# Fixing the order of VectorE, ScalarE and GpSimd in two stages of a two-layer transformer kernel

## The chip, the cores and the metric

The kernel runs on one core of one Trainium2 chip. The core has a matrix engine (TensorE, PE in the profile, with its weight loads listed as PEld), a vector engine (VectorE, DVE), an activation engine (ScalarE, ACT), a general engine (GpSimd, POOL) and SyncE (SP), which issues most transfers. Every engine works through its own list of instructions in order; semaphores hold an instruction until what it needs is done. The metric is the device time of one execution in microseconds (us); the times before are 2042.14, 2020.98 and 2023.09, median 2023.09. They spread over 1%.

## The reference

The input `x` is 8 batch items of 512 tokens with 256 features. Two layers follow each other, each with a conditioning in front of its attention and of its feed-forward part:

```python
x = x + L0_attn(L0_cond(x, c), ...)        # modulated attention; biased causal attention, 16 heads
x = x + L0_ffn(L0_cond2(x, ids, ...), ...) # conditioning by tables and a small network; 8 experts, top 2
x = x + L1_attn(L1_cond(x, c), ...)        # adapter with weights from c; linear attention with exp features
x = x + L1_ffn(L1_cond2(x, c, ...), ...)   # weights from c; 8-bit product with a scale per token
```

The second conditioning of layer 0, cut to its core, and the routing of its experts:

```python
h = ln(x, pw_g[pid], pw_b[pid]); h = ln(h, cp_g[cid], cp_b[cid])
t = ln(x, tm_g[cid], tm_b[cid]); s = ln(x, ms_g[mid], ms_b[mid])
m, n, r = (x + mlp_ln(state) for each of three states)
cat = concat([w0*h, w1*t, w2*m, w3*n, w4*r, w5*s])
xc = ln(silu(cat @ W1 + b1) @ W2 + b2)
probs = softmax(xc @ Wr + br); p, e = top_k(probs, 2)
pos = (how many earlier tokens of the item chose the same expert); keep = pos < 80
buf[e, item, pos] += xc                    # 80 slots per expert and item
y = relu(buf @ W1[e] + b1[e]) @ W2[e] + b2[e]
out = sum over the two choices of p * keep * y[slot]
```

## The kernel before

Python code traces the whole program as a list of instructions; a planner then sorts each engine's instructions by what it expects of their readiness, subject to the data they need, and places the semaphores. Three things take freedom from it. Every matrix product goes through `pmm` or a transpose through `ptr`, and both tie each product to the one before it, so that PE runs in the order of the source everywhere. A few GpSimd and VectorE operations are told to keep their order among themselves (`tc.keep_in_program_order`). And the first stage calls `in_order`, which adds an ordering edge, without a semaphore, from each instruction of VectorE, ScalarE or GpSimd to the next one of the same engine in the traced list:

```python
def in_order(start):
    last = {}
    for i in nc.cur_bb.bb.instructions[start:]:
        if i.engine not in (DVE, Activation, Pool):   # names shortened
            continue
        if i.engine in last:
            tc.add_manual_dep(i, last[i.engine].name, ...)
        last[i.engine] = i
```

The program has four stages. `stage_a1` is the first conditioning and attention. `stage_a2` is the second conditioning and the routing. `stage_b` runs the eight experts. `stage_c` runs layer 1. Tokens lie 128 to a tile, so there are 32 tiles, four to a batch item.

`stage_a2` handles two tiles (a "unit") per pass of its loop, 16 units in all, and is pipelined by hand over passes `it` = 1 to 22. In pass `it`, unit u = it is normalized, v = it - 1 is transposed, w = it - 2 goes through the first product of the network, y = it - 3 through the second, z = it - 4 through the router's product. The source traces a pass in this order:

1. statistics of unit u (`bn`, lines 1194 and 1195), `turn(v, 0)`: eight transposes on PE of four tensors (the input, ss, hh, tt) and two ScalarE copies into `cat`;
2. `layer2(y)` on PE, then on VectorE the addition of the bias (xc, line 1388) and the statistics of xc;
3. `inverse`: ScalarE takes a square root (line 1200), VectorE the reciprocal (1201) and the negated mean nmr (1340);
4. `normalize(u)`: ScalarE makes xh (1328); GpSimd makes tt and ss (1331, 1332) and issues the next unit's gathers from the tables (1142) between them;
5. `layer1(w, 0)` on PE; the four scalings of xc on VectorE (1400, 1401);
6. `pathway(u)`: four VectorE operations make hh (1347, 1348), then their statistics and a second `inverse` with its own square root and reciprocal;
7. `logits_turn(z)`: PE transposes of xc and a ScalarE copy xcT (1244); `turn(v, 1)`;
8. in an even pass from 6 on, `choose`: thirteen small VectorE operations that pick the two experts of each token and make `r_M` (1275); in an odd pass from 7 on, `one_hot` for the first two tiles of a batch item (1309, 1310, two operations of 640 columns for a tile);
9. `layer1(w, 1)` on PE, `silu(w)` on ScalarE (1228);
10. `compartment(u)`: four VectorE operations finish hh (1358, 1359);
11. `logits(z)` on PE, and their addition lg on VectorE (1252);
12. in an even pass, `places`: a product with `r_M` on PE (pos_ps) and ten small VectorE operations (1291 to 1302), then `dispatch(·, 1)`; in an odd pass, `one_hot` for the other two tiles, then `dispatch(·, 0)`.

`dispatch` is eight products on PE, for each half of the slots one for each of the four tiles in turn, so that it needs all four one-hots of the item; ScalarE copies the result (1319). The transposes of `turn(v, i)` read the hh of tile i alone.

In front of the loop the first two units are done as a "lead"; it is traced after the first stage and runs beside its tail, and its gathers are tied behind operations of the first stage's last round.

`stage_c` loops over nine rounds. In one round, the front half of batch item b (adapter, projections, features kf and qf, key-value products) is interleaved with the back half of item b - 1 (attention's division, output product, the quantized product). What matters here: `kfeatures` applies exp on ScalarE and an addition on VectorE to four tiles (1710, 1711), `values` adds a bias to the products v_ps (cv, 1694), `z` quantizes one tile in six VectorE operations (1817 to 1825), `qfeatures` is like `kfeatures` (1725, 1726), `keyvalues_turned` copies one half on VectorE (1752) and one on ScalarE (1753), `turn_q` copies a transposed tile on ScalarE (qzT, 1832), and `acc` is the quantized product with its scaling (r, 1840). In these two stages `small` and `ps_o` tiles in PSUM come from pools of three and two, so that a product can wait for the release of an earlier one.

Of the kernel before, what the change touches and what calls it, by code (L numbers as in the profile page):

```python
# [45 lines left out]
def tile_kernel(ctx: ExitStack, tc: tile.TileContext, t, out):  # L46
# [1394 lines left out]
        nc.vector.tensor_tensor(gates[:, 1], gates[:, 1], keep[:, 1], ALU.mult)  # L1441

    with ExitStack() as sub:
        stage_a2(sub)

# [461 lines left out]
                g.acc(3)  # L1909

    with ExitStack() as sub:
        stage_c(sub)


def pack(i):
# [70 lines left out]
def build(nc, arrays, out_ap):  # L1986
    t = {k: nc.dram_tensor("in_" + k, a.shape, mybir.dt.from_np(a.dtype), kind="ExternalInput").ap()
         for k, a in arrays.items()}
    with tile.TileContext(nc) as tc:
        tile_kernel(tc, t, out_ap)  # L1990
# [12 lines left out]
```

## Time and profile before

| what | value |
|---|---|
| median of the runs (lowest to highest) | 2023.09 us (2020.98 to 2042.14) |
| profiled execution: its own time, and the span in it | 2027.99 us, 2025.8 us |
| busy over the span: PE, DVE, ACT, POOL | 1827.9 (90%), 1140.9 (56%), 744.3 (37%), 689.2 (34%) |
| mean granted PE clock | 0.938 |
| PE of the second conditioning | 1030 to 1318, 288 us: PE busy 272.5, DVE 245.8 |
| PE of the experts | 1318 to 1617, 299 us: PE busy 294.4, DVE 67.3 |
| PE of the last stage | 1617 to 2026, 409 us: PE busy 369.8, DVE 254.5 |

A busy share is a mean over stages with different limits, so the stages are read one by one. The profile's times come from one execution; its own time is 2.2 us more than the span from its first instruction to its last. A time in brackets behind an instruction is how long its engine stood idle in front of it and what ended that. The durations of consecutive VectorE rows overlap by some 0.08 us, so sums in the text go from start to start. The granted clock of PE is given as a share of full speed.

### The profile page before, as it was taken

Reading aid. Unit: us, or ns where it says so; the run is one execution under the profiler, and the core shown is the slowest. Engines: PE = TensorE matmul, PEld = TensorE weight load, DVE = VectorE, ACT = ScalarE, POOL = GpSimd, SP = SyncE. Lnnn points to the kernel's source line nnn. Section 1 sums busy time; section 2 is a strip of 40 time slices with the busy share of each in tenths; the row PEclk is TensorE's granted clock in tenths of the full one; section 3 lists DMA queues with packets and bytes.
Section 4 is the critical chain, followed back from the end, with each engine's and each line's share of the span. In section 5 each row is a group of like instructions: output and inputs, shape, how many; then the busy total and the mean of one; then the engine's idle time right before and its main releaser. Section 6 shows DMA issues by size and latency. Waiting matters only on the chain.

```text
span 2025.8 us, 46400 instructions
## 1 busy us (share of the span) xinstructions
PE 1827.9 (90%) x19638; PEld 1258.0 (62%) x19658; DVE 1140.9 (56%) x2646; ACT 744.3 (37%) x1444; POOL 689.2 (34%) x1071
## 2 busy tenths in 40 slices
PE   6789898988999898988689999999999889999997
PEld 3446566555656566555468788777777645555554
DVE  3455656555655556565569898622221246666666
ACT  3425344353545344344445445311110023333332
POOL 3324332333434332332277555000000244444422
PEclk7698899999999998998789999999999989999999
DMA  4110101111020101101254334222322211111100
GB/s 132 39 42 7 39 17 44 33 44 32 7 65 7 59 7 45 37 22 53 100 193 150 124 125 137 87 78 92 105 70 74 51 44 31 34 32 35 35 12 22
DMA packets 102107, 119.72 MB, mean 59 GB/s; under 512 B 45350, under 2 KB 82332, under 8 KB 101772
## 3 DMA queue, kind: packets, MB, share of 16 engines
q1 hardware_dynamic: 91660, 74.82, 12.0%
q0 software_dynamic: 10240, 41.95, 6.5%
q8 instruction: 154, 2.52, 0.5%
q14 instruction: 53, 0.43, 0.1%
HBM read 94.46 MB, written 22.27 MB: 58 GB/s over the span
## 4 chain that ended last, share of the span: by engine, by line
PE 36%; DVE 12%; ACT 2%; POOL 2%; issue 2%; DMA 1%; SPq 0%; POOLq 0%; ACTq 0%; DVEq 0%
PE h_ps L87 7%; PE y_ps L87 6%; PE qf_ps L87 2%; PE kv_ps L87 2%; PE k_ps L87 1%; PE wo_ps L87 1%; PE dsp L87 1%; PE q_ps L87 1%; PE z_ps L87 1%; DVE s L1194 1%; DVE o1h L1310 1%; PE kf_ps L87 1%; PE hid_ps L87 1%; PE down_ps L87 1%; PE v_ps L87 1%
## 5 line engine op out<-in xcount | busy, mean ns | idle before, releaser
L745 ACT ACTIVATE eo<-o 128x384 f32<-128x384 f32 x256 | 111.8, 489 | 282.1 <-PE o L87 226.7
L722 POOL TENSOR_SCALAR_AFFINE_SELECT ed<-ed 128x512 f32<-128x512 f32 x128 | 78.9, 639 | 339.4 <-ACT ed L721 339.2
L87 PE MATMUL h_ps<-bufT,w 128*128 128x320 f32 x512 | 141.9, 438 | 0.0
L87 PE MATMUL y_ps<-w,hT 128*128 128x256 f32 x640 | 139.4, 379 | 0.0
L87 PEld LDWEIGHTS y_ps<-w,hT 128*128 128x128 f32 x640 | 121.6, 190 | 17.4
L87 PEld LDWEIGHTS h_ps<-bufT,w 128*128 128x128 f32 x512 | 97.9, 192 | 43.7 <-DVE us L1557 3.4
L1529 ACT ACTIVATE hT<-h_ps,w_b 128x320 f32<-128x320 f32 x64 | 33.8, 527 | 245.8 <-PE h_ps L87 245.8
L1594 POOL MEMSET bn<- 128x512 f32 x1 | 0.5, 525 | 342.7 <-PE h_ps L87 342.7
L87 PE MATMUL hid_ps<-cat,wx 128*128 128x256 f32 x512 | 116.4, 381 | 0.0
L604 DVE SCALAR_TENSOR_TENSOR kts<-kt_ps,w_bkp,fk 128x512 f32<-128x512 f32 x32 | 24.0, 751 | 160.1 <-PE kt_ps L87 160.1
L87 PEld LDWEIGHTS hid_ps<-cat,wx 128*128 128x128 f32 x512 | 96.7, 192 | 12.8
L639 DVE TENSOR_REDUCE mx<-mx_d 128x4 f32<-128x512 f32 x128 | 82.4, 686 | 33.8 <-PE mx_d L87 29.8
L1531 DVE TENSOR_SCALAR hT<-h_ps,w_b 128x320 f32<-128x320 f32 x64 | 35.3, 551 | 114.9 <-PE h_ps L87 114.9
L87 PE MATMUL o<-qts,kts 32*128 32x128 f32 (+1 forms) x768 | 96.3, 346 | 0.0
L706 DVE TENSOR_TENSOR sd<-sd,wt 128x512 f32<-128x512 f32 x128 | 82.1, 687 | 16.7 <-PE sd L87 10.4
L87 PE MATMUL sd<-qt,ktc 32*128 32x128 f32 x1024 | 87.2, 305 | 3.3 <-ACT ed L721 3.3
L87 PE MATMUL o<-mt,onesb 32*128 32x384 bf16 (+2 forms) x384 | 59.0, 286 | 33.0 <-DVE mx L639 25.2
L87 PEld LDWEIGHTS sd<-qt,ktc 32*128 32x128 f32 x1024 | 71.7, 204 | 23.7 <-issue 16.8
L87 PE MATMUL sd<-qt,kts 16*128 16x128 f32 x1024 | 81.0, 294 | 0.0
L87 PEld LDWEIGHTS sd<-qt,kts 16*128 16x128 f32 x1024 | 70.9, 200 | 16.0 <-issue 15.5
L1538 DVE TENSOR_TENSOR ye<-y_ps,bc_b 128x256 f32<-128x256 f32 x40 | 17.0, 424 | 107.4 <-PE y_ps L87 107.4
L87 PEld LDWEIGHTS o<-qts,kts 32*128 32x128 f32 x768 | 75.9, 201 | 0.2
(423 smaller groups left out, 4596.6 us busy)
## 6 DMA issues: line engine op xcount, KB each, us to landing
w<-in_W SPq DMA_DIRECT2D x16, 1024.0 KB
xT<-in_xT SPq DMA_DIRECT2D x8, 512.0 KB
kxd<-kxF SPq DMA_DIRECT2D x8, 512.0 KB
raw<-kxd SPq DMA_DIRECT2D x64, 64.0 KB
xr<-in_x SPq DMA_DIRECT2D x8, 512.0 KB
ond<-on SPq DMA_DIRECT2D x64, 64.0 KB
oT<-ond SPq DMA_DIRECT2D x8, 512.0 KB
x1d<-xr SPq DMA_DIRECT2D x8, 512.0 KB
```

The source lines that it names most:

```text
L87: pin(nc.tensor.matmul(*a, **kw))
L604: nc.vector.scalar_tensor_tensor(kts.rearrange("p (j k) -> p j k", k=P), ps.rearrange("p (j k) -> p j k", k=P), bkp[:, g:g + 1], fk[:, g]. ...
L639: nc.vector.tensor_reduce(mx[:, g, 0:4], d[g].rearrange("p (j k) -> p j k", k=P), AX.X, ALU.max)
L706: nc.vector.tensor_tensor(d3, d3, wt[:, self.hg * 4 + g].unsqueeze(1).to_broadcast([P, NT, P]), ALU.mult)
L722: zeroed.append(nc.gpsimd.affine_select(e, e, pattern=[[0, NT], [1, P]], compare_op=ALU.is_ge, fill=0.0, base=0, channel_multiplier=-1))
L745: nc.scalar.activation(e, self.o[g][:, :3 * P], AF.Exp)
L1194: nc.vector.bn_stats(s6, x)
L1310: nc.vector.scalar_tensor_tensor(o1, slot, sd[:, 1, j:j + 1], o1, ALU.is_equal, ALU.add)
L1529: nc.scalar.activation(dst, ps, AF.Relu, bias=b1[:, e, hc:hc + 1])
L1531: nc.vector.tensor_scalar(dst, ps, b1[:, e, hc:hc + 1], 0.0, ALU.add, ALU.max)
L1538: nc.vector.tensor_tensor(ye[:n], ps[:n], b2[:n, e * D:(e + 1) * D], ALU.add)
L1594: nc.gpsimd.memset(bn8, -0.125)
```

## The change

The change marks the start of the traced list in front of the second conditioning and of the last stage, and calls `in_order` behind each. VectorE, ScalarE and GpSimd then keep, inside these stages, the order in which the source traces their instructions; GpSimd's gathers are instructions of GpSimd and are tied too. PE, SyncE, the first stage and the experts' stage are left as they are, and no instruction is added or removed.

```diff
     with ExitStack() as sub:
+        begun = traced()
         stage_a2(sub)
+        in_order(begun)
...
     with ExitStack() as sub:
+        begun = traced()
         stage_c(sub)
+        in_order(begun)
```

## The prediction

> **What bounds the kernel now.** I read the window sums by stage first, then the waits of each engine, then the timeline of one pass of the second conditioning. The columns of the sums are window, length, then busy time of PE, PEld, DVE, ACT, POOL, the granted PE clock, DMA share and rate.
>
> ```profile
> 1030.00:1318.00 288.00, 272.51 (x1411) 227.92 (x1410) 245.84 (x681) 136.89 (x238) 148.54 (x174) 0.98 0.41 139
> 1617.00:2026.00 409.00, 369.83 (x3504) 222.93 (x3504) 254.49 (x638) 129.88 (x256) 166.71 (x196) 0.96 0.12 31
> 1181.00:1214.40 33.40, 33.40 (x180) 28.55 (x179) 32.61 (x90) 16.81 (x30) 20.97 (x24) 1.00 0.37 127
> 1119.30:1126.10 6.80, 5.58 (x16) 4.63 (x17) 2.96 (x13) 1.87 (x2) 1.71 (x2) 0.50 0.62 225
> ```
>
> The second conditioning has PE 1030 to 1318, the last stage 1617 to the end. The third line is one steady pair of passes (one batch item): PE is busy all 33.4 us and DVE 32.6. Two engines are full at once, which works only if neither waits for the other. The fourth line I use below. Now the order, in the timeline (start, duration, instruction):
>
> ```profile
> 1203.50 0.20 DVE L1291 TENSOR_TENSOR r_oh<-r_oh,pos_ps 128x64 f32<-128x64 f32 x1
> 1205.36 0.64 DVE L1302 TENSOR_TENSOR r_sd<-r_sd,keep 128x8 f32<-128x8 f32 x1
> 1206.04 1.09 DVE L1309 TENSOR_SCALAR o1h<-slot,r_sd 128x640 f32<-128x640 f32 x1
> 1208.24 3.62 PE L87 MATMUL hid_ps<-cat,wx 128*128 128x256 f32 x16
> 1208.89 1.68 DVE L1310 SCALAR_TENSOR_TENSOR o1h<-slot,r_sd,o1h 128x640 f32<-128x640 f32 x2
> 1211.07 0.88 DVE L1310 SCALAR_TENSOR_TENSOR o1h<-slot,r_sd,o1h 128x640 f32<-128x640 f32 x1
> 1211.87 0.75 DVE L1388 TENSOR_TENSOR xc<-xc_ps,bc_int_b 128x256 f32<-128x256 f32 x2
> 1213.53 0.30 ACT L1200 ACTIVATE rs<-mv,eps 128x4 f32<-128x4 f32 x1 [4.55 <-DVE mv L1195]
> 1217.27 4.55 PE L87 MATMUL dsp<-o1h,xc 128*128 128x320 f32 x16
> ```
>
> The planner puts all four one-hots (L1309/L1310) directly behind the places, ahead of the next pass's xc (L1388), though the source has two in the middle of that pass (L1413) and two at its end (L1426). The last is ready at 1211.95, and `dispatch` reads it from 1217.27: 5.3 us of reserve. It likewise lifts `choose` ahead of xc, and fills each wait for ACT's square root with other work.
>
> **The change part by part.** No instruction is added or removed. PE is pinned in source order in both. What changes is which DVE and ACT instructions stand behind a waiting one. I walk both kinds of pass in source order, zero at the end of `layer2`. "Choosing" is an even `it`, "one-hot" an odd one.
>
> *DVE, both kinds.* xc adds and statistics take 1.54 from 1211.87; in source order each aggregate stands directly behind its own statistics, so two overlaps of about 0.1 go and 0.1 passes from PE: done at 1.85. Now nothing stands between the aggregate and the reciprocal: 0.30 of ACT and some 0.15 of hand-over, idle, to 2.3. Reciprocal and nmr 2.55. Four xc operations (0.88 + 0.88 in the timeline) 4.3. Four hh operations (1.29 + 1.28 at 1215.29) 6.9. Their statistics 7.9. A second idle root 8.35, reciprocal 8.45.
> *Choosing pass:* choose 4.1 (1188.98 to 1193.05) 12.55; compartment 3.1 (1.39 + 1.72) 15.65; lg; places 2.5 (1203.50 to 1206.04).
> *One-hot pass:* two one-hots 2.9 (four take 5.83, 1206.04 to 1211.87) 11.35; compartment 14.45; lg; the other two 17.4.
> *PE.* layer1 3.45, xc transposes 0.44, turn 0.88, layer1 3.45: 8.2. Logits need the xcT copy, which in source order is queued on ACT behind the second root (8.3), so 8.95 to 9.8. In the one-hot pass, dispatch waits for the fourth one-hot, then has five of eight products at 0.56 left: 17.5 to 20.3. Behind that, turn 0.88 and layer2 1.74: **22.95**. In the choosing pass, `places`' product waits for choose: 12.65 to 13.6, dispatch 4.45, turn, layer2: **20.7**. A pair is 43.65 against 33.4: +10.2.
>
> *Clock.* The idle stretches are new. In the one-hot pass PE does 1.1 us of work in the 7.7 us from 9.8; in the choosing pass 0.85 in the 4.4 from 8.2. The trace has both kinds once. PE waited 4.28 us for an hh at 1120.5 and the clock stood at 0.50 from 1119.3 to 1126.1; layer2 then took 3.62 instead of 1.89, layer1 4.26 instead of 3.62: 2.4 lost.
>
> ```profile
> 1120.52 0.66 PE L90 MATMUL cat_t<-ident,hh 128*128 128x128 f32 x2 [4.28 <-DVE hh L1359]
> 1121.40 3.62 PE L87 MATMUL xc_ps<-w_int_W,hid 128*128 128x256 f32 x8
> 1189.60 1.89 PE L87 MATMUL xc_ps<-w_int_W,hid 128*128 128x256 f32 x8
> ```
>
> The other is layer2 at 1098.7, which took 3.7, so 1.8 lost, after gaps of only about 1 us between short products. [...] By the second row thin work is enough. I follow the row: 2.4 in each one-hot pass and half of 1.8 in each choosing pass (bounds 0 and twice that), so 25.35 and 21.6: 47 a pair.
>
> *Sum of the stage.* From `layer2` in pass 6 (ends 1085.2) to pass 16 (1257.8) the kernel now takes 172.6. In order: pass 6 has no dispatch yet and ends 16.9 after its layer2 (turn follows the first half of compartment at 14.1); five one-hot passes 126.7; four choosing passes 86.4: 230, **+57**. From pass 16 on nothing normalizes and GpSimd is idle; the rows there are shorter (choose 2.5, places 1.3, four one-hots 5.4). The same walk gives 16.3, 15.7 and then 35.1 to the end, 67.1 against 60.5 now: **+7**. Passes 3 to 5 have neither choose nor one-hot; turn follows half of compartment at 10.0, layer2 ends at 12.7 against 12.4: **+1**. The lead in front of 1030 lies beside the first stage's tail; its normalization keeps GpSimd to about 1049 in either order (24 products of 0.77 and 8 gathers of 1.0 from 1022.8), so lifting gathers no longer, or again, is nothing; without that cover a late gather costs up to 4. I take 0, bounds -3 and +4.
>
> *Last stage.* Its order is nearly the source's already. Three spots differ each round, and there DVE is 62% busy.
>
> ```profile
> 1791.44 1.13 PE L87 MATMUL z_ps<-wz,x3T 128*128 128x256 f32 x4 [0.57 <-DVE cv L1694]
> 1803.80 0.40 ACT L1832 COPY qzT<-q_t 128x256 bf16<-128x256 bf16 x1
> 1804.25 0.39 PE L87 MATMUL acc_ps<-wqb,qzT 128*128 128x256 bf16 x2 [1.30 <-ACT qzT L1832]
> 1804.60 0.41 DVE L1752 COPY kv<-kv_t 64x256 f32<-64x256 f32 x1
> 1804.93 0.61 DVE L1726 TENSOR_SCALAR qf<-qf 128x512 f32<-128x512 f32 x1
> 1805.04 0.37 ACT L1753 COPY kv<-kv_t 64x256 f32<-64x256 f32 x1 [0.84 <-DVE kv L1752]
> ```
>
> In source order kv (L1752) follows the last qf, ACT's half of kv follows that, and qzT comes behind it: from 1803.80 to about 1806. PE's acc stands 2 us later; the next product waited until 1805.98 anyway, so 1.1 remains. And kf's fourth operation goes ahead of cv, for which PE already waits: 0.36 at two places. z(0) and z(1) no longer interleave, which delays only products several microseconds later: nothing. Seven rounds of 1.8 are 13; part falls into PE's other waits. I take **+8**, bounds -3 and +14. ACT's and GpSimd's other moves here are single swaps of preparations: nothing.
>
> Against the profiled execution: 2025.8 of span and 2.2 around it, 2028.0, plus 57 + 7 + 1 + 8 = 73 gives 2101. That execution lies 4.9 above the median of the runs, so the forecast is 2023.1 + 73, rounded to **2095**.
>
> **The rivals.**
> *Nothing is lost (2023; 3%).* [...] Work per pair stays 32.6 for DVE and 33.4 for PE, [...]; equally if the planner's order came out as the source's. Against it: at 98% on DVE and all of PE, each wait for the other adds, and the loop xc, one-hot, dispatch, turn, layer2, xc runs through both.
> *Faster (2008; 3%).* PE idles 15.5 of 288 now. Part is the planner's doing: at 1115 to 1120 it had a later `choose` ahead of an hh that PE wanted. Source order always serves compartment before the next pass's choose. It wins up to the 15.5 if the fourth one-hot is ready when logits end, at 9.8 of a pass; I have it at 17.4, and nothing short of 7 us nearer decides for this rival.
> *Half the loss (2057; 14%).* DVE's two-input rows stretch beside GpSimd: choose is 4.1 with it, 2.5 without; places 2.5 and 1.3; an hh operation 0.65 and 0.43. If the idle time moves the two engines apart, up to 6 of a pair's 13.6 come back and the clock stays up: +26 for these passes, +8 for the others and none in the last stage.
> *More (2120; 8%).* [...] the last stage takes its 14 and falls too.
> The forecast itself has 72%.
>
> **How the numbers follow.** The walk's uncertain terms (clock 0 to twice, last stage -3 to 14, lead -3 to 4) put the likeliest case at 2070 to 2115. Reaching into the half loss and the upper case gives 2056 to 2118. The three runs spread over 1%, and about 1% is what can be told from no change; faster by that 0.03, within it 0.03, slower 0.94.
>
> **What would show it.** Right: steady pairs of 43 to 48 us; in them PE waiting for o1h at dispatch in one-hot passes and for r_M at pos_ps in choosing ones; idle DVE in front of both reciprocals (L1201) and of xc (L1388); clock dips in this stage; PE at some 80% of it; qzT behind kv in the last stage. Experts' stage unchanged at 299. Wrong: pairs under 38, or the loss lying in the lead (DVE of the first stage stuck behind a gather), or in the last stage by more than 15.

## The result, and the profile after

The changed kernel takes 2159.03 us (median of four runs, 2147.18 to 2163.18) against 2025.34 (2020.98 to 2042.14): a ratio of 1.063, 95% interval 1.056 to 1.069. The forecast was 2095, range 2056 to 2118. The sign was right and the size was not: 73 us were forecast, about 134 came. The profiled execution took 2157.32 us with a span of 2155.3, so the spans differ by 129.5, and its stages are compared below. The mean clock fell from 0.938 to 0.915.

The window sums of the changed kernel, in the columns shown for before (window, length, busy PE, PEld, DVE, ACT, POOL, clock, DMA share, rate), are for the second conditioning, the last stage and one steady pair of passes:

```profile
1030.00:1431.30 401.30, 320.85 (x1429) 251.94 (x1430) 262.61 (x680) 134.79 (x237) 157.18 (x183) 0.86 0.31 102
1729.00:2155.30 426.30, 369.92 (x3504) 222.41 (x3504) 263.69 (x637) 130.87 (x256) 164.87 (x196) 0.95 0.11 30
1223.80:1275.10 51.30, 40.43 (x177) 31.16 (x178) 35.84 (x89) 16.92 (x30) 21.36 (x24) 0.83 0.24 83
```

A pair takes 51.3 us where it took 33.4. Two things grew inside it although no instruction was added: PE is busy 40.4 us where it was 33.4, at a clock of 0.83 where it was 1.00 (a slower clock, not more work), and DVE is busy 35.8 where it was 32.6.

The table sets out the span of before and after from landmarks of PE: the first `cat_t` transpose, the ends of `layer2` (a row "passes 6 to 15" runs from its end in pass 6 to its end in pass 16), the last `dsp`, the first `dgb_ps`.

| us | before | after | difference | forecast |
|---|---|---|---|---|
| up to the first `cat_t` | 1030.4 | 1034.6 | +4.2 | 0 |
| lead, to `layer2` of pass 3 | 18.4 | 26.0 | +7.6 | 0 |
| passes 3 to 5 | 36.4 | 47.3 | +10.9 | +1 |
| passes 6 to 15 | 172.6 | 252.9 | +80.3 | +57 |
| pass 16 to the last `dsp` | 60.5 | 70.6 | +10.1 | +7 |
| experts | 298.9 | 297.7 | -1.2 | 0 |
| last stage | 408.6 | 426.2 | +17.6 | +8 |

The first row is not the change's: in the kernels run here that point lies anywhere between 1024 and 1047. The waits in the second conditioning of the changed kernel (who <- for whom: total, times, longest) are those that were foreseen, with two more at the lead:

```profile
DVE xc L1388 <- PE xc_ps L87: 80.9, 16, 7.7
PE lg_ps L87 <- ACT xcT L1244: 26.9, 14, 2.4
PE dsp L87 <- DVE o1h L1310: 20.9, 19, 2.3
PE pos_ps L87 <- DVE r_M L1275: 17.4, 6, 3.1
DVE rs L1201 <- ACT rs L1200: 15.7, 31, 4.8
PE cat_t L90 <- POOL ss L1332: 9.9, 1, 9.9
DVE hh L1347 <- DMA g<-in_tab_pw,ids: 7.4, 2, 6.8
```

The timeline of one steady one-hot pass after the change, to be read beside the lines of before (zero of the walk, the end of `layer2`, is at 1232.75):

```profile
1236.19 0.95 DVE L1400 SCALAR_TENSOR_TENSOR xc<-xc,mv,bc_int_g 128x256 f32<-128x256 f32 x1
1242.42 0.17 DVE L1201 RECIPROCAL rs<-rs 128x2 f32<-128x2 f32 x1 [0.36 <-ACT rs L1200]
1242.91 1.06 PE L87 MATMUL lg_ps<-w_Wr,xcT 128*128 128x8 f32 x8 [1.94 <-ACT xcT L1244]
1244.80 1.80 DVE L1310 SCALAR_TENSOR_TENSOR o1h<-slot,r_sd,o1h 128x640 f32<-128x640 f32 x1
1245.17 0.73 POOL L1331 TENSOR_TENSOR ss<-xh,g 128x256 f32<-128x256 f32 x1
1245.98 1.20 POOL L1332 TENSOR_TENSOR ss<-ss,g 128x256 f32<-128x256 f32 x1
1250.42 5.87 PE L87 MATMUL dsp<-o1h,xc 128*128 128x320 f32 x12 [2.33 <-DVE o1h L1310]
1258.93 0.75 DVE L1388 TENSOR_TENSOR xc<-xc_ps,bc_int_b 128x256 f32<-128x256 f32 x2 [6.10 <-PE xc_ps L87]
```

VectorE waits 6.1 us for `layer2` at the end, and PE has waited for VectorE before that: neither is full any more. The first row and the fourth to sixth hold what the forecast missed. The second one-hot's row of line 1310 takes 1.80 us, twice its 0.88 elsewhere, while GpSimd's two products run (one of these is stretched as well, from 0.72 to 1.20). So here a VectorE and a GpSimd row, which lie side by side in the new order, each take longer, by 0.92 and 0.48 us. And in the choosing pass:

```profile
1263.49 3.62 PE L87 MATMUL hid_ps<-cat,wx 128*128 128x256 f32 x16
1269.06 1.06 PE L87 MATMUL lg_ps<-w_Wr,xcT 128*128 128x8 f32 x8 [1.95 <-ACT xcT L1244]
1272.98 0.19 DVE L1275 TENSOR_TENSOR r_M<-r_oh 128x32 f32<-128x32 f32 x1
1273.22 0.63 PE L87 MATMUL pos_ps<-r_M,tri 128*128 128x32 f32 x2 [3.11 <-DVE r_M L1275]
1273.67 1.43 PE L87 MATMUL pos_ps<-r_M,ones 128*128 128x24 f32 x6
1274.95 6.46 PE L87 MATMUL dsp<-o1h,xc 128*128 128x320 f32 x16
```

PE has waited 3.1 us for the choice; the sixteen dispatch products behind it then take 6.46 us where the row of before took 4.55. The clock was at half from 1272.0 to 1278.8.

### The profile page after: what moved, and what is told of

Same layout as the page of the kernel before. It is cut to its first block, busy times and chain, and to the rows that moved or that the text cites. A ratio compares the mean times of both kernels' runs of the same rounds, so it can differ in the third digit from the quotient of the medians.

```text
span 2155.3 us, 46374 instructions
## 1 busy us (share of the span) xinstructions
PE 1874.2 (87%) x19658; PEld 1278.8 (59%) x19658; DVE 1168.7 (54%) x2646; ACT 740.8 (34%) x1440; POOL 688.8 (32%) x1071
## 5 line engine op out<-in xcount | busy, mean ns | idle before, releaser
L87 PEld LDWEIGHTS y_ps<-w,hT 128*128 128x128 f32 x640 | 121.6, 190 | 17.4
L87 PE MATMUL dsp<-o1h,xc 128*128 128x320 f32 x256 | 104.4, 563 | 20.9 <-DVE o1h L1310 20.9
L604 DVE SCALAR_TENSOR_TENSOR kts<-kt_ps,w_bkp,fk 128x512 f32<-128x512 f32 x32 | 24.0, 751 | 160.5 <-PE kt_ps L87 160.5
L87 PEld LDWEIGHTS dsp<-o1h,xc 128*128 128x128 f32 x256 | 59.3, 246 | 59.9 <-DVE o1h L1310 37.3
L1533 DVE TENSOR_SCALAR hT<-h_ps,w_b 128x320 f32<-128x320 f32 x64 | 35.1, 549 | 103.9 <-PE h_ps L87 103.9
L706 DVE TENSOR_TENSOR sd<-sd,wt 128x512 f32<-128x512 f32 x128 | 82.1, 686 | 16.4 <-PE sd L87 11.0
```

Source lines behind the costliest of these rows:

```text
L87: pin(nc.tensor.matmul(*a, **kw))
L604: nc.vector.scalar_tensor_tensor(kts.rearrange("p (j k) -> p j k", k=P), ps.rearrange("p (j k) -> p j k", k=P), bkp[:, g:g + 1], fk[:, g]. ...
L706: nc.vector.tensor_tensor(d3, d3, wt[:, self.hg * 4 + g].unsqueeze(1).to_broadcast([P, NT, P]), ALU.mult)
L1533: nc.vector.tensor_scalar(dst, ps, b1[:, e, hc:hc + 1], 0.0, ALU.add, ALU.max)
```

## The experiments

"Passes 6 to 15" and the other stage times are taken as in the table above. A single run beside one of before is given as such; its stages, not its total, carry the reading.

**Where: each half of the change alone.**

```diff
+        begun = traced()
         stage_a2(sub)
+        in_order(begun)
```

The second kernel has the same three lines round `stage_c(sub)` and not round `stage_a2(sub)`.

> The order is fixed in the second conditioning alone; the last stage is left to the planner. Measured for both: span +129.5 us, of which 113 lie between the start of the first stage's tail and the last dispatch, 17.7 behind the first dgb product of the last stage. Theory (the two stages add, nothing of the loss is shared): 2025 + 113 = 2138, 2132 to 2144. Rival (the last stage is slower because of what the first leaves behind, its gathers or the clock): nearly the whole 2150 to 2159.

> The order is fixed in the last stage alone. Theory (loss of its own, mostly PE's acc waiting for a qzT that is queued behind kv, and z waiting for cv): rounds of 51.3 us as in the changed kernel, 2025 + 18 = 2043, 2038 to 2048. Rival (the loss comes with the second conditioning): 2022 to 2030.

The second conditioning alone: ratio 1.049 (1.041 to 1.057), lead 25.7, passes 3 to 5 46.9, passes 6 to 15 253.2, tail 70.6: all of the change's loss there. The last stage alone: 1.0105 (1.0065 to 1.0145), stage 425.6 and the second conditioning as before. The two losses are separate and add up. Both totals lie outside what was expected for them (medians 2128.31 and 2055.56 us), on a chip where the kernel before took 2017 to 2044; the stages carry the reading here too.

**Is it the order, or the fixing of it?** The order that the planner had found was written into the source of the second conditioning (statistics of both tiles ahead of both aggregates, xc's first scalings and `compartment`'s first operations in the gaps of the square roots, all four one-hots behind `places`, `choose` at the end of the pass before its own, gathers among the products of the lead) and then fixed by the same `in_order`. The core:

```diff
-            if r % 2 and 0 < r < NU:
-                choose(r // 2)
-            elif r > 1 and r - 1 < NU:
-                one_hot(r // 2 - 1, (0, 1))
...
+                one_hot(r // 2, range(NT))
...
+            if r >= 0 and r % 2 == 0 and r < NU:
+                choose(r // 2)
```

> The second conditioning alone in order, with the planner's own steady order written into the source: one-hots behind places, choose at the end of the pass before, xcT and the cat copies ahead of the second root, the first scaling between root and reciprocal, pairs of independent operations side by side, the next unit's gathers between the lead's products. Theory (the order itself is the whole cause): pairs of 33 to 34 us and 2015 to 2035. Rival (the ordering edges, or the tie of the engines' lists to the source, cost by themselves): pairs above 38, 2060 or more.

Ratio 1.002 (0.9994 to 1.0047), passes 6 to 15 in 175.0 us, steady pairs in 33.0 to 36.4. So fixing an order costs nothing that can be measured; this order does. It is not better than the kernel before either.

**Which engine's list?** `in_order` was given an engine to hold, the others left to the planner.

```diff
-    def in_order(start):
+    def in_order(start, only=None):
...
+            if only and i.engine != only:
+                continue
```

> In the second conditioning VectorE alone is held to the source's order; ScalarE and GpSimd are left to the planner, and so is the last stage. Theory (VectorE's list carries the loss: late one-hots, late choose, idle roots): passes 6 to 15 take 235 to 253 us (172.6 before, 253.2 with all three engines held), PE's waits for logits behind xcT gone. Rival (ScalarE's order carries it, by xcT behind the second root): under 200.

> In the second conditioning ScalarE alone is held to the source's order. Theory (VectorE's list carries the loss): xcT stands behind the second root, which comes about 6 us behind the first xc in the planner's order of VectorE too, and PE waits 1 to 2 us for it in a pass: passes 6 to 15 take 175 to 195 us. Rival (ScalarE carries it): over 220.

VectorE alone: 2126.44 (before 2038.29 beside it), passes 6 to 15 in 253.9: the whole loss of these passes, just above the 235 to 253 expected. In front of them about half is left (lead 21.0, passes 3 to 5 42.8), so that part needs the other lists too. PE's waits in the second conditioning name the mechanism:

```profile
PE dsp L89 <- DVE o1h L1312: 32.7, 19, 4.6
PE pos_ps L89 <- DVE r_M L1277: 31.7, 6, 5.3
```

ScalarE alone: 2053.05 us, passes 6 to 15 in 181.2, the wait for xcT 15.4 us. The late xcT of the forecast is there, but in the changed kernel it lies mostly inside the time by which VectorE is late anyway.

**The one-hots in the middle of the pass.** All four put back directly behind `places`, in the held order.

```diff
-                one_hot(r // 2 - 1, (0, 1))
+                pass
...
+                one_hot(r // 2, range(NT))
...
-                one_hot(r // 2 - 1, (2, 3))
```

> As with the second conditioning alone in order, but the source calls all four one-hots of an item directly behind its places, one pass earlier; nothing else is moved. Theory (in one-hot passes the dispatch waits for the last one-hot): a one-hot pass falls from 26.1 to about 18 us, the choosing pass stays near 25, a pair 43 to 44 instead of 51.3; total 2138 - 37 = about 2100, 2090 to 2110. Rival (PE's waits for logits behind the xcT copy, 26.9 us in all, are what counts, and the one-hot waits only stand in their place): pairs of 48 or more, 2120 to 2138.

Ratio 1.038 (1.028 to 1.048); passes 6 to 15 in 234.0. The one-hot passes from 9 on fall from 26.2 to between 20.9 and 22.9, the choosing passes stay at about 25. Pairs of 45.7 to 47.6 us lie between the theory's 43 to 44 and the rival's 48 or more: moving the one-hots alone gives back 18.9 of the 80.3.

**The clock.** Products that nothing reads were put in the idle stretches of PE (five of 320 columns ahead of `places`' product, nine among the first four dispatch products of a one-hot pass), to keep the clock up.

```diff
+            fill = ps_d.tile([P, NS // 2], F32, tag="d", name="fill")
+            for _ in range(5):
+                pmm(fill, ones, slot[:, :NS // 2], start=True, stop=True)
...
+                    if c == 0 and g == 0:
+                        for _ in range((0, 2, 5, 2)[j]):
+                            pmm(both[1], xcs[b * NT + j][:, 0:P], slot[:, :NS // 2], start=True, stop=True)
```

> All three engines held in the second conditioning. PE gets extra products into PSUM that nothing reads, where it stands idle now: nine inside the dispatch of a one-hot pass and five in front of the places' product of a choosing pass; they need nothing that is late. Theory (the half clock makes a good part of a pass): half-clock time in this stage falls from 119 to under 40 us, the dispatch of a choosing pass from 6.4 to 4.55, the rest of the other one from 4.5 to 2.8, and passes 6 to 15 from 253 to about 230. Rival (dispatch is slow there for another reason, the clock only accompanies it): 248 or more.

The time at half clock in this stage falls from 116.1 to 54.6 us (under 40 was expected), passes 6 to 15 from 252.9 to 238.7. The steady choosing pass falls from 25.1 to 22.4, the one-hot pass only from 26.1 to 25.3, and the tail grows by 15, where the fillers are not hidden. So the clock is worth at least 14 of the 80 us, 2.7 in a choosing pass. It didn't reach the expected 230, and the clock still fell in the one-hot passes; what the rest of the dips costs this run doesn't give.

**GpSimd beside VectorE.** The products of lines 1331 and 1332 are left out, which leaves the scaling by the t and s tables out of the computation; GpSimd keeps its gathers, and `turn` transposes xh in their place. Once in the changed second conditioning, once in the planner's order.

```diff
-                        tc.keep_in_program_order(nc.gpsimd.tensor_tensor(o[i], xh[i], gcm[:, q], ALU.mult))
-                        tc.keep_in_program_order(nc.gpsimd.tensor_tensor(o[i], o[i], gcm[:, q + 1], ALU.add))
...
-                    hh_[2 * u + i], ss_[2 * u + i], tt_[2 * u + i] = hh[i], ss[i], tt[i]
+                    hh_[2 * u + i], ss_[2 * u + i], tt_[2 * u + i] = hh[i], xh[i], xh[i]
```

> All three engines held in the second conditioning, GpSimd's four products and sums for each tile left out: the third and sixth parts of the concatenation are then xh without the table's scaling and shift, so that part of the computation is missing. GpSimd keeps its gathers. Theory (VectorE's two-input rows stretch beside GpSimd, some 1.5 us a pass more than in the walk): the second reciprocal lies at 8.4 to 8.7 of a pass instead of 9.8, and passes 6 to 15 take 253 - 15 = 238 or a little less. Rival (the stretch lies beside other waits): 248 or more.

> The kernel before (planner's order) with the sixteen-per-pair GpSimd products of the second conditioning (lines 1331 and 1332, the scaling of the t and s tables) left out, so its output is not the reference's. Read against the source-order kernel without them, whose pair of passes fell from 51.3 to about 40.7 us. Theory (the planner's order keeps PE busy whatever VectorE's rows cost, so that GpSimd's slowing of them is hidden and is paid for only once the order is fixed): the steady pair stays at 33 to 33.4 us and passes 6 to 15 at 170 to 173. Rival (VectorE at 32.6 of 33.4 us is a bound of its own before as well, and its shorter rows gain): pair 30 to 31.5, passes 6 to 15 at 156 to 164. Either way the lead in front of layer 2 may be shorter by some us.

The window sums of one steady pair, first in the source's order, then in the planner's:

```profile
1170.60:1211.35 40.75, 36.36 (x178) 29.07 (x177) 27.80 (x89) 16.93 (x30) 7.57 (x8) 0.92 0.33 104
```

```profile
1180.05:1212.98 32.93, 32.93 (x178) 28.14 (x177) 25.39 (x89) 17.17 (x30) 7.95 (x8) 1.00 0.41 129
```

In the source's order a pair falls from 51.3 to 40.75 without the products: DVE's busy time from 35.8 to 27.8 and PE's from 40.4 to 36.4, since the clock is up more often (half clock 44.4 us in the stage, from 116.1). Passes 6 to 15 take 200.6, where I had expected 238, so this was undervalued even once the result was known. In the planner's order VectorE's work falls nearly as far, from 32.6 to 25.4, and the steady pair gains nothing from one end of `layer2` to the next (16.0 and 16.9 in both kernels): PE was the bound and all of it was hidden. That is the theory's value. But passes 6 to 15 as a whole gain 12.1 (172.6 to 160.5, the rival's value), nearly all of it in passes 6 to 8, where the choice of experts and the one-hots begin (57.3 to 45.7): PE's waits there for hh (5.4 us) and ss (0.8) are gone, and so are the 10.2 us of half clock. The four kernels split the loss of passes 6 to 15: the order alone costs 200.6 - 160.5 = 40.1 us; that GpSimd's products now slow a VectorE on which PE waits costs 52.3 where it cost 12.1, another 40.2. The clock lies in both parts and is not to be added to them: half clock in these ten passes is 92.5 us in the changed kernel, 34.1 without the products, and 10.2 and 0.0 in the planner's order. The runs without the products are single ones.

VectorE's groups of the one-hot's second half and of xc's and hh's operations in one stretch (1100 to 1240) show it row by row (count, busy, mean ns), first two of them in the kernel before, then in the changed kernel, then in the changed kernel without the products:

```profile
L1310 DVE SCALAR_TENSOR_TENSOR o1h<-slot,r_sd,o1h 128x640 f32<-128x640 f32 x16 | 13.8, 880 | 0.2
L1400 DVE SCALAR_TENSOR_TENSOR xc<-xc,mv,bc_int_g 128x256 f32<-128x256 f32 x16 | 6.9, 472 | 0.0
```

```profile
L1310 DVE SCALAR_TENSOR_TENSOR o1h<-slot,r_sd,o1h 128x640 f32<-128x640 f32 x8 | 9.6, 1199 | 0.3
L1348 DVE TENSOR_TENSOR hh<-hh,g 128x256 f32<-128x256 f32 x11 | 9.4, 850 | 0.4
L1400 DVE SCALAR_TENSOR_TENSOR xc<-xc,mv,bc_int_g 128x256 f32<-128x256 f32 x12 | 8.6, 715 | 0.0
L1194 DVE BATCH_NORM_STATS2 s<-xc 128x6 f32<-128x256 f32 x12 | 4.9, 406 | 0.0
```

```profile
L1310 DVE SCALAR_TENSOR_TENSOR o1h<-slot,r_sd,o1h 128x640 f32<-128x640 f32 x14 | 12.4, 884 | 0.5
L1346 DVE TENSOR_TENSOR hh<-hh,g 128x256 f32<-128x256 f32 x14 | 5.9, 425 | 0.5
L1398 DVE SCALAR_TENSOR_TENSOR xc<-xc,mv,bc_int_g 128x256 f32<-128x256 f32 x14 | 6.7, 478 | 0.0
L1194 DVE BATCH_NORM_STATS2 s<-xc 128x6 f32<-128x256 f32 x14 | 5.7, 406 | 0.0
```

Without GpSimd's products these operations with two inputs in SBUF shrink to flat values (the one-hot's from 1199 to 884 ns, hh's from 850 to 425, xc's from 715 to 478), and the statistics, with one input, take 406 ns in both. The 1.80 us row above loses 0.92 us, GpSimd's first product ends 1.10 after the row's start, and the second takes 0.48 more than its 0.72. By what means the two engines slow each other was not shown, nor why the row, listed as the first of them to start, is the one that loses most. Before, the mean of the xc row was 0.47 us, since the planner had it clear of GpSimd's products; in the source's order it starts with them, behind the same nmr.

**The lead.** The gathers of unit 2 put among the lead's products again, in the held order.

```diff
-        normalize(lead, rs, negated_means(mv, rs, 4))
+        normalize(lead, rs, negated_means(mv, rs, 4), gather(LEAD))
...
-            ahead = gather(it + 1) if LEAD <= it + 1 < NU else None
+            ahead = gather(it + 1) if LEAD < it + 1 < NU else None
```

> All three engines held in the second conditioning; the gathers of the third unit are traced between the lead's products instead of behind all sixteen. Theory (they start 13 us later in the changed kernel, and the first hh of the loop waits for them): from the first transpose to the end of the first layer2 18 to 19 us instead of 25.7, the rest as with all three engines held. Rival (the lead is late for VectorE's or ScalarE's order): 24 or more.

The lead falls from 26.0 to 20.9, more than half of its loss though not to the 18 to 19 that were expected, and pass 3 grows from 14.4 to 16.5: up to pass 6, 3.0 of the 18.5 us are won. What it was in the changed kernel, from the timeline:

```profile
1039.94 1.00 POOL L1142 DMA_INDIRECT g<-in_tab_pw,ids  x1
...
1047.19 0.42 DVE L1347 TENSOR_TENSOR hh<-xh,g 128x256 f32<-128x256 f32 x1 [6.77 <-DMA g<-in_tab_pw,ids]
...
1055.62 0.69 PE L90 MATMUL cat_t<-ident,ss 128*128 128x128 f32 x2 [9.87 <-POOL ss L1332]
```

The gathers stand behind all sixteen products of the lead. The first hh of unit 2 then waits until 7.3 us after the first issue, VectorE with it, and everything behind: PE stands 9.9 us for an ss that GpSimd makes only afterwards. In steady passes (1150 to 1250) the gathers land a median of 3.3 and 4.8 us after their issue, here 7.2 and 8.9, where they meet the loads that SyncE issues at the start of this stage; the window sum has the DMA share at 0.99 and 328 GB/s:

```profile
1038.00:1050.00 12.00, 7.75 (x41) 6.62 (x39) 2.44 (x8) 3.09 (x5) 5.55 (x7) 1.00 0.99 328
```

With the gathers among the products the first is issued ahead of those loads and lands in 3.2 us. That the loads make the difference is read from these figures; no run moved the loads alone.

**The last stage.** ScalarE's list alone and VectorE's alone held there, as above; and all three held with `qzT` put ahead of the kv copies in the source.

```diff
-                f.keyvalues_turned()
             if o:
                 g.turn_q(3)
+            if f:
+                f.keyvalues_turned()
+            if o:
                 g.acc(2)
```

> In the last stage ScalarE alone is held to the source's order: its one repeated move is qzT behind kv. The second conditioning is left to the planner. Theory (acc's wait for qzT is most of the loss): rounds of 49.5 to 51 us instead of 47.4, PE's waits for qzT 15 us or more in all. Rival (VectorE's moves, cv behind the fourth kf and kv behind the fourth qf, are the loss): rounds under 48.5.

> The kernel before with VectorE's order alone held in the last stage (ScalarE and GpSimd there, and the whole second conditioning, are left to the planner). With ScalarE's alone held a round stayed at 47.8 us though acc waited 19.5 us for qzT; with all three held it takes 51.3, and with qzT put ahead of the kv copy in the source about 49.4. Theory (VectorE's list carries it: cv behind the fourth kf addition, kv behind the fourth qf addition): rounds of 50 to 51.3 us, the stage 418 to 426, span near 2040 to 2045. Rival (only both lists together make it, since qzT is late only when ScalarE waits for a late kv): rounds under 48.5, the stage under 412.

> The last stage alone is held to the source's order, with the copy of the fourth transposed tile traced ahead of kv's copies. Theory (acc's wait for qzT behind kv is most of the loss): rounds of 48 to 49 us instead of 51.3, PE's waits for qzT under 12 us in all. Rival (cv and the rest of VectorE's order): 50.5 or more.

The stage as a whole varies from 399.8 to 413.6 us over ten kernels here whose last stage is left to the planner, so I use the seven rounds between the first and the eighth kvT, and PE's waits in the stage, which vary less:

| held in the last stage | seven rounds, us | PE for cv | PE for qzT |
|---|---|---|---|
| nothing (ten kernels) | 328.0 to 335.2 | 3.8 to 3.9 | 6.8 to 8.2 |
| ScalarE | 334.1 | 3.8 | 19.5 |
| VectorE | 341.2 | 10.8 | 7.0 |
| all, `qzT` first | 343.0 | 10.8 | 9.3 |
| all (alone; with the other stage) | 351.3; 352.0 | 10.8 | 23.0 |

(The waits of the first row were read in six of the ten.) PE's waits in the kernel before, with ScalarE alone held, then in the changed kernel:

```profile
PE acc_ps L87 <- ACT qzT L1832: 8.2, 7, 1.3
PE z_ps L87 <- DVE cv L1694: 3.8, 7, 0.6
```

```profile
PE acc_ps L89 <- ACT qzT L1834: 19.5, 8, 2.9
PE z_ps L89 <- DVE cv L1696: 3.8, 7, 0.6
```

```profile
PE acc_ps L87 <- ACT qzT L1834: 23.0, 7, 3.5
PE z_ps L87 <- DVE cv L1696: 10.8, 7, 1.7
```

VectorE's list alone costs 7 us against the median of the ten (334.0), 6 against the slowest of them, and PE's wait for cv grows by 7.0 with it; that lies between the two theories of its run. A late `qzT` alone costs nothing that shows, though PE waits 11 us more for it, so the theory of the run with ScalarE's list was wrong. PE's waits for r at the product behind (`ugb_ps`), 5.7 us before, are gone there; where the other half went is open. With VectorE's list held too, `qzT` stands behind a kv that is itself behind the fourth qf, and that costs another 8 to 11 us; either freeing ScalarE or putting `qzT` first gives them back.

## Why the prediction was right in sign and wrong in size

Right: PE and VectorE were both full, so that any wait of one for the other adds; the rival of no loss rested on their unchanged work (32.6 and 33.4 us a pair), and the 80 us that passes 6 to 15 lost say otherwise. The waits came where they were named (o1h, r_M, xcT, both reciprocals, xc), the clock dipped in every pass, the experts' stage stayed. The rival "half the loss" had two-input rows shrink as the engines move apart; VectorE's busy time of a pair grew instead, from 32.6 to 35.8 us (means from 1100 to 1240: the one-hot's second half from 880 to 1199 ns, xc's first scaling from 472 to 715, while `compartment`'s second operation fell from 872 to 543). Nearest to what came was the rival "more", with more lost to the clock in every pass and 14 us in the last stage, and that stops at 2120. Two of the prediction's own signs speak against it: a steady pair was to take 43 to 48 us and takes 51.3, and a last stage longer by more than 15 was to mean wrong; it is longer by 17.6.

The steps that failed:

*"I follow the row: 2.4 in each one-hot pass and half of 1.8 in each choosing pass", and VectorE's durations taken from the rows of before.* The walk gave 21.6 for a choosing pass; it takes 25.1 to 25.5. Of the 3.6, 1.7 are VectorE's: xc's four operations 2.7 for 1.8, hh's 3.0 for 2.6, choose 4.4 for 4.1, so that PE gets r_M at 14.3 instead of 12.65. The places' product at 1.8 instead of 0.95 and dispatch at 6.46 instead of 4.55 lose 2.7 to the clock, where 0.9 was allowed. The filler run, with the clock mostly up, has 22.4 for this pass: the walk's 20.7 and those 1.7. For one-hot passes the walk gave 25.35 and 26.2 is measured, which is near by luck: the fourth one-hot is ready at 19.0 instead of 17.4, and the five products behind it lose 1.5 to the clock, where 2.4 was allowed for the pass. Pass 6 had no clock term at all: 21.2 for 16.9, since `turn` begins 2 us later and it and `layer2` lose 2.5 to the half clock. Four choosing passes (+14.5), five one-hot passes (+4.2) and pass 6 (+4.3) make the 23 by which 230 fell short of 252.9.

*"Passes 3 to 5 ... ends at 12.7 against 12.4: +1."* They take 14.4, 16.5 and 16.4. Without GpSimd's products the same order takes 12.2, 12.7 and 12.7, which is the walk's number: about 10 us are GpSimd and the clock that falls with it (6.5 us at half clock in these passes, none before).

*"so lifting gathers no longer, or again, is nothing ... I take 0, bounds -3 and +4."* The cover was not there: with the gathers last, GpSimd has issued them at 1044.7, stands 6.3 us until unit 2's rows have come and ends that unit's products at 1060.9, where it ended them at 1046.8 before. From issue to use a gather took 7 us and more, and "up to 4" was allowed for a late one. The lead lost 7.6.

*"Seven rounds of 1.8 are 13; part falls into PE's other waits. I take +8."* The estimate of each place was near, and the discount from 13 to 8 was wrong. With both lists held the wait for qzT grows by 14.8 and that for r falls by 5.7, so 1.3 a round for the 1.1 of the walk; the wait for cv grows by 7.0, so 1.0 for 0.72. That makes 16 for the 13, and the stage grew by 17.6. The discount holds for ScalarE's list alone, where 11 us of waiting cost nothing that shows.

*The tail, +7,* was 10.1: its two passes came as walked (16.0 and 15.9), what follows took 38.7 for 35.1, with 6.8 us at half clock where the walk had none. Together the misses are 23 + 10 + 7.6 + 10 + 3, and 3 of noise in front of the stage and in the experts': 57 of 129.5 - 73.

## What to carry to other kernels

Where two engines are both full, take the durations for the new order from how the rows lie in the new order: a two-input VectorE row that starts with GpSimd's products costs here up to twice its row elsewhere (line 1310, 1.80 us for 0.88; a small one of 32 columns in `choose`, line 1267, 0.74 for 0.19), and it costs time only where PE then waits for it (7.2 us less of VectorE's work in a pair left the planner's steady pair at 32.9 us). Price the clock for every pass with a new gap, not for half of them: thin work in front of a long product came with a slow long product here (6.46 us for 4.55). And of an engine that is busy anyway, ask which of its instructions has moved to the end, above all if it issues transfers, and what these transfers will meet there (here gathers, 7.2 and 8.9 us to landing for 3.3 and 4.8).

## What was not expected of the hardware

The clock fell in every steady pass, and after stops of PE that were short: in the choosing pass above PE had run 1.06 us of logits in the 4.9 us up to 1272.0, and its longest stop until then was 1.95. Half clock held for 6.8 us in steady choosing passes and for 10.2 in one-hot passes, 116 us of this stage's 401. GpSimd's products cost the second conditioning about 18 us before the change (lead 4.2, passes 3 to 5 1.8, passes 6 to 15 12.1) and about 70 after it (9.1, 9.6 and 52.3, less 1.0 in the tail), with the same sixteen products a pair.
